# The second attention of a hybrid block: the last sums of squares of a group given later, the query tiles of a head from the longest down, and whole products in the last group

## The chip, the cores and the metric

The kernel runs on one core of a Trainium2 chip. The metric is the device time of one launch in microseconds, as the median of several runs. TensorE (PE in the profile) multiplies matrices into PSUM, VectorE (DVE), ScalarE (ACT) and GpSimd (POOL) work on vectors, SyncE (SP) starts the loads and stores. Each engine runs its own list of instructions in order and waits for others at semaphores.

## The reference

All is in fp32, with T = 1024 tokens of C = 512 channels. The block is four residual steps:

```
x = x + attention_a(layernorm(x))     # 32 heads of 16, rotary, causal
x = x + ffn(layernorm(x))             # base product, 2 of 8 low-rank experts
x = x + attention_b(layernorm(x))     # 32 query heads of 128, 8 key/value heads
x = x + ffn(layernorm(x))
```

Only attention B is changed. It computes

```
q = rmsnorm(x @ Wq.T) * qw            # 32 heads
k = rmsnorm(x @ Wk.T) * kw            # 8 heads, each for 4 query heads
v = x @ Wv.T
s = q k / sqrt(128) + slope * (key - query),  -1e30 where key > query
out = softmax(s) v;   result = out @ Wo.T
```

The mask is causal, so a query tile i (128 queries) sees the keys 0 to (i+1)*128: tile 7 is eight times as wide as tile 0.

## The kernel before

**Tiles and stages.** Attention B runs from about 500 to 1611 us of the profile. Its loop goes over 8 groups g (one key/value head each), 4 query heads hh of the group, and 8 query tiles i. For each tile:

- `softmax(g, hh, i)`: TensorE gives the scores s in one or two pieces of at most 512 keys (L791) into the pool `ps_s`, which has two PSUM buffers. VectorE multiplies each piece by the queries' norm factor rq and adds the distance (L793, "p"), takes the row maximum over the whole width (L797, "nm") and scales it (L798). ScalarE takes the exponent and its sum (L800), VectorE the reciprocal (L802), GpSimd scales p by it (L803).
- `columns(hh, p, i)`, two tiles later (`LAG = 2`): VectorE transposes p in 32x32 blocks, the first five key tiles into `PT` (L818, "pT") and the others into `TT` (L824, "tT"). `PT` is one buffer that all heads use; `TT` has a place for each of the four heads.
- `product(g, hh, i0, i1)`: TensorE multiplies the columns in PT of query tiles i0 to i1 by v, in matmuls that use 32 rows of the array each, four side by side (L835 through `by_groups`, "o"); ScalarE copies the result to oT (L860). It is called after the head's last tile.
- `product_rest(g, heads)`: the same for the key tiles 5 to 7 in TT, for several heads in one matmul ("or"), which VectorE adds to oT (L876). In groups 0 to 6 it is called once for all four heads, at the next group's start.

**What fills between.** While the softmax of group g goes on, TensorE is given the other work in small units. A generator `fill` yields after each: `project_kv(g+1)` makes keys and values of the next group in 8 units (four matmuls "kv" L700 each, then ScalarE's squares L708 and VectorE's copies k L709 and v L710), `project_o(g-1)` multiplies the previous group's oT by Wo and adds to x in 32 units (L642 "wo", addition L647), and `project_q(g+1)` makes the next group's queries in 32 units (L745 "pq"; ScalarE's squares L754, "qT" on VectorE L755), with one transposition of keys (L99 "tp_k", L728) between. All of these, and `sum_squares`, use the pool `ps_m` with two PSUM buffers.

`sum_squares(g, hh, sq)` sums the squares of a head's queries by four matmuls with ones (L771 "st"), transposes the sums on VectorE (L775 "by"), scales them (L779 "rq"), and takes the power on GpSimd. `project_q` calls it for head hh when it is two matmuls into head hh + 1, and for the last head at its own end, between two further yields.

**What sets the order.** After tile n of 32 the loop takes units of the fill until `done` reaches `due`, which is `units * n // 32`: an equal share for each tile, with `units` 74 (42 in group 0, which has no project_o). A scheduler then places the instructions of each engine, within what data and buffers allow, so that neighbours can change places. The last group has no next group: its fill is project_o(6) during heads 0 and 1, then project_o(7) for heads 0 and 1 together and for head 2; the last head's part of project_o runs inside the ffn that follows. In this group each head makes its product in two halves, tiles 0 to 3 when tile 3 is there and 4 to 7 when tile 7 is there, and its own product_rest.

Of the kernel before, what the change touches and what calls it, by code (L numbers as in the profile page):

```python
# [18 lines left out]
NT = T // P  # L19
# [16 lines left out]
HKV = 8  # L36
GRP = HB // HKV
# [27 lines left out]
class Block:  # L65
# [557 lines left out]
    def attention_b(self, ctx, wo_pool, WqT, WkT, WvT, WoT, qw, kw, xnT, missing, ffn_weights):  # L623
# [12 lines left out]
        oTs = {}  # L636
# [13 lines left out]
        with ExitStack() as ctx:  # L650
# [70 lines left out]
                        nc.gpsimd.tensor_scalar(k_sb[:, a, :], k_sb[:, a, :], rk[:, a : a + 1], 1.0, ALU.mult, ALU.mult)  # L721
                    later.append((g, half, k_sb, kT))

            later = []

            def k_columns(g, half, k_sb, kT):
                ps = self.transpose4(ps_m, [k_sb[:, a, :] for a in range(4)], f"k{g}{half}", tag="m")
                nc.scalar.activation(  # L728
                    kT[:, half * QC : (half + 1) * QC], ps.rearrange("p a b -> p (a b)"), AF.Copy, scale=kw_sb
                )  # L730

            def project_q(g, wq):

                qTs[g] = []
                rqs[g] = []
                sums = []
                for hh in range(GRP):
                    qT = qp.tile([P, T], F32, tag="qT", name=f"qT{g}_{hh}")
                    qTs[g].append(qT)
                    rqs[g].append(sm.tile([P, NT], F32, tag="rq", name=f"rq{g}_{hh}", bufs=6))  # L740
                    for qc in range(NQC):
                        cols = slice(qc * QC, (qc + 1) * QC)
                        ps = ps_m.tile([P, QC], F32, tag="m", name=f"pq{g}_{hh}_{qc}")
                        for kc in range(KC):
                            nc.tensor.matmul(  # L745
                                ps, lhsT=wq[:, kc, hh * DB : (hh + 1) * DB], rhs=xnT[:, kc, cols], start=(kc == 0), stop=(kc == KC - 1)
                            )
                            if kc < KC - 1:
                                yield
                            if kc == 1 and sums:  # L750
                                sum_squares(g, *sums.pop(0))
                        if qc == 0:
                            sq = work.tile([P, T], F32, tag="w", name=f"qsq{g}_{hh}", bufs=1)
                        nc.scalar.activation(sq[:, cols], ps, AF.Square)  # L754
                        nc.vector.tensor_scalar_mul(qT[:, cols], ps, qw_sb)  # L755
                        yield
                        while later:
                            k_columns(*later.pop(0))
                    sums.append((hh, sq))
                yield  # L760
                sum_squares(g, *sums.pop(0))
                yield

            def sum_squares(g, hh, squares):

                rq = rqs[g][hh]
                st = ps_m.tile([P, QC], F32, tag="m", name=f"st{g}_{hh}")[:, : NT * B]
                for a, sq in enumerate(squares.rearrange("p (i a c) -> a p i c", a=P // B, c=B)):  # L770
                    nc.tensor.matmul(  # L771
                        st[a * B : (a + 1) * B, :].rearrange("p (i c) -> p i c", c=B), lhsT=ones, rhs=sq, start=True, stop=True
                    )
                by_token = work.tile([P, NT, B], F32, tag="st", name=f"by{g}_{hh}", bufs=1)
                nc.vector.transpose(by_token.rearrange("p i c -> p (i c)"), st)  # L775


                s2 = slopes[g * GRP + hh] ** 2
                nc.vector.tensor_scalar(rq, by_token[:, :, 0], s2, DB * RMS_EPS * s2, ALU.mult, ALU.add)  # L779
                self.rsqrt(rq, rq, [NT])  # L780
# [62 lines left out]
            def queries(t, i0, i1):  # L843

                return t[:, i0 * P : i1 * P].rearrange("p (i a c) -> p a i c", a=NB, c=B)

            def product(g, hh, i0, i1):

                n = i1 - i0
                o = ps_o.tile([P, NB, QC], F32, tag="o", name=f"o{g}_{hh}_{i0}")  # L850
                by_groups(
                    g,
                    o,
                    lambda o, j: o[:, max(j - i0, 0) * B : n * B],
                    range(min(JS, i1)),
                    lambda j, rows, ks: PT[rows, (NT - 1) * j + max(j, i0) : (NT - 1) * j + i1, ks],
                )
                if i0 == 0:
                    oTs[g, hh] = otp.tile([P, T], F32, tag="oT", name=f"oT{g}_{hh}")
                nc.scalar.copy(queries(oTs[g, hh], i0, i1), o[:, :, : n * B].rearrange("p a (i c) -> p a i c", c=B))  # L860

            def product_rest(g, heads):

                n, h0 = len(heads), heads[0]
                o = ps_o.tile([P, NB, QC], F32, tag="o", name=f"or{g}_{h0}")
                by_groups(
                    g,
                    o,
                    lambda o, j: o[:, : n * JT * B].rearrange("p (h q) -> p h q", h=n)[:, :, (j - JS) * B :],
                    range(JS, NT),  # L870
                    lambda j, rows, ks: TT[rows, h0 : h0 + n, (JT - 1) * (j - JS) + j - JS : (JT - 1) * (j - JS) + JT, ks],
                )
                for h in heads:
                    to = queries(oTs[g, h], JS, NT)
                    more = o[:, :, (h - h0) * JT * B : (h - h0 + 1) * JT * B].rearrange("p a (i c) -> p a i c", c=B)
                    nc.vector.tensor_add(to, to, more)  # L876

            def in_turn(*gens):
                for g in gens:
                    yield from g  # L880
# [7 lines left out]
            heads = list(range(GRP))  # L888
            rest = []

            def finish(g, hh, i, p):
                while rest:
                    product_rest(*rest.pop(0))
                columns(hh, p, i)
                if g == HKV - 1:

                    if i == NT // 2 - 1:
                        product(g, hh, 0, NT // 2)
                    elif i == NT - 1:
                        product(g, hh, NT // 2, NT)  # L900
                        product_rest(g, [hh])
                elif i == NT - 1:
                    product(g, hh, 0, NT)
                    if hh == GRP - 1:
                        rest.append((g, heads))

            for g in range(HKV):


                last = g == HKV - 1  # L910
                parts = []
                if not last:
                    wq, wkv = load_qkv(g + 1)
                    parts.append(project_kv(g + 1, wkv))
                    parts.append(project_q(g + 1, wq))
                if g:
                    parts.insert(-1, project_o(g - 1, wo, heads, ps_m, "m"))
                fill = in_turn(*parts)
                units = 74 if g else 42
                done = 0  # L920
                for hh in range(GRP):
                    if g and hh == 2:
                        if last:
                            for _ in fill:
                                pass
                        wo = load_o(g)
                        if last:
                            fill = in_turn(project_o(g, wo, [0, 1], ps_m, "m"), project_o(g, wo, [2], ps_m, "m"))
                    for i in range(NT):
                        p = softmax(g, hh, i)  # L930
                        n = hh * NT + i + 1
                        if not last:
                            due = units * n // (GRP * NT)
                        elif hh < 2:
                            due = max(0, (n - 2) * 32 // 14)
                        else:
                            due = 32 + max(0, 2 * (n - 19)) if n < 27 else 48 + (n - 27)
                        while done < due:
                            next(fill, None)
                            done += 1  # L940
                        pending.append((g, hh, i, p))
                        if len(pending) > LAG:
                            finish(*pending.pop(0))
                    if last and hh == GRP - 1:
                        for item in pending:
                            next(fill, None)
                            finish(*item)
                for _ in fill:
                    pass
                if g == HKV - 2:  # L950

                    self.load_ffn(wp, nc.sync, ("wkv", "wq"), *ffn_weights)
# [156 lines left out]
```

## Time and profile before

| | |
|---|---|
| runs | 1683.14, 1683.34, 1686.43 us; median 1683.34 |
| profiled execution, its own time | 1683.11 us |
| its span in the trace | 1681.3 us |
| TensorE busy, share of the span | 1652.6 us, 98% |
| VectorE | 1103.0 us, 66% |
| ScalarE | 542.1 us, 32% |
| GpSimd | 347.8 us, 21% |
| L835 o and or, L745 pq, L791 s on the chain | 13% and 3%, 12%, 12% |
| product and rest records of L835 before the last group | 160 a head, 96 a group of four heads |

The span is what the trace covers, from the first instruction to the last; the launch's own time is a little longer. A busy TensorE is not TensorE at its peak: matmuls are pipelined, and the profile models their ends, so two rows of matmuls overlap a little. An fp32 matmul shows as two records. A timeline row gives start, length, engine and line, the operation with its output and inputs, how many records it holds, and in brackets the idle time before it with what ended that. A row of the waits gives the instruction that waited, the one that it waited for, total us, times, and the longest. A row of the groups by shape gives busy time, mean ns of one, and idle time before with what ended most of it.

### The profile page before, as it was taken

The page shows a single profiled execution, that of the slowest core. Times are in us where ns is not written, and L with a number is a line of the kernel's source. Part 1 is how long each engine was busy: PE and PEld are TensorE (multiplying, and loading weights), DVE is VectorE, ACT ScalarE, POOL GpSimd, SP SyncE. Part 2 cuts the span into 40 slices and gives each one's busy share as a digit, 9 for nine tenths or more (in the row PEclk, how much of TensorE's full clock was granted, in tenths as well). Part 3 has the DMA queues.
Part 4 walks back from the last instruction along what each step waited for, and adds up shares of the span by engine and source line. Part 5 has one row for each costly group of instructions (what it writes and reads, how often), then busy time and mean ns, then how long its engine had stood idle before and what let it go on. Part 6 is the DMA issues. An engine that isn't in the chain of part 4 may idle for free.

```text
span 1681.3 us, 32166 instructions
## 1 busy us (share of the span) xinstructions
PE 1652.6 (98%) x13016; PEld 940.7 (56%) x13016; DVE 1103.0 (66%) x2856; ACT 542.1 (32%) x1217; POOL 347.8 (21%) x508
## 2 busy tenths in 40 slices
PE   9999999999999999999999999999999999999988
PEld 5544444344555667556655665756655665566654
DVE  3556666662653886776677667676677766776773
ACT  2315555555111332233233223223223322322220
POOL 2000000000312332222123212222222321221140
PEclk9999999999999999999999999999999999999999
DMA  5000000001003201100200200110020020000001
GB/s 195 1 1 2 2 2 2 2 2 38 2 24 88 65 2 41 49 26 26 64 26 26 61 30 1 51 38 26 26 64 26 26 71 26 1 27 27 2 1 50
DMA packets 60868, 52.06 MB, mean 31 GB/s; under 512 B 5744, under 2 KB 47472, under 8 KB 60720
## 3 DMA queue, kind: packets, MB, share of 16 engines
q1 hardware_dynamic: 59408, 46.06, 9.2%
q0 software_dynamic: 784, 2.90, 0.4%
q8 instruction: 102, 1.67, 0.4%
q10 hardware_dynamic: 528, 1.05, 0.2%
q14 instruction: 46, 0.38, 0.1%
HBM read 30.98 MB, written 2.10 MB: 20 GB/s over the span
## 4 chain that ended last, share of the span: by engine, by line
PE 87%; DVE 10%; ACT 1%; POOL 1%; issue 1%; DVEq 0%; ACTq 0%; POOLq 0%
PE o L835 13%; PE pq L745 12%; PE s L791 12%; PE wo L642 9%; PE sT L354 7%; PE kv L700 7%; PE oT L389 5%; PE s L302 4%; PE pm_f L599 3%; PE or L835 3%; DVE p L793 3%; DVE nm L797 2%; DVE pT L818 2%; PE pj_v L179 2%; PE pm_ao L993 2%; PE pj_k L179 2%
## 5 line engine op out<-in xcount | busy, mean ns | idle before, releaser
L803 POOL TENSOR_SCALAR p<-p,rs 128x128 f32<-128x128 f32 (+7 forms) x256 | 190.8, 747 | 750.6 <-DVE rs L802 685.7
L800 ACT ACTIVATE p<-p,nm 128x128 f32<-128x128 f32 (+7 forms) x256 | 198.1, 774 | 453.4 <-DVE nm L798 443.0
L793 DVE SCALAR_TENSOR_TENSOR p<-s,rq,rel 128x512 f32<-128x512 f32 (+3 forms) x384 | 227.1, 605 | 119.4 <-PE s L791 118.8
L791 PE MATMUL s<-kT,qT 128*128 128x512 f32 (+3 forms) x768 | 294.8, 492 | 1.8 <-DVE p L793 1.5
L745 PE MATMUL pq<-xnTb,wq 128*128 128x512 f32 x512 | 246.2, 599 | 0.0
L642 PE MATMUL wo<-wo,oT 128*128 128x512 f32 x512 | 241.8, 594 | 3.4 <-DVE x L647 1.9
L791 PEld LDWEIGHTS s<-kT,qT 128*128 128x128 f32 x768 | 141.2, 190 | 165.8 <-issue 126.1
L835 PEld LDWEIGHTS o<-pT,va 32*128 32x128 f32 x5632 | 215.7, 185 | 28.5 <-DVE rs L802 11.8
L835 PE MATMUL o<-pT,va 32*128 32x128 f32 (+7 forms) x5632 | 224.6, 313 | 0.8
L818 DVE STREAM_TRANSPOSE pT<-p 128x640 f32<-128x640 f32 (+4 forms) x256 | 172.1, 673 | 73.1 <-PE o L835 54.7
L374 ACT ACTIVATE p<-sT 128x512 f32<-128x512 f32 (+1 forms) x320 | 157.5, 555 | 113.4 <-PE sT L372 70.9
L797 DVE TENSOR_REDUCE nm<-p 128x1 f32<-128x128 f32 (+7 forms) x256 | 188.2, 736 | 3.6
L302 PE MATMUL s<-kT,qT 32*128 32x512 f32 (+3 forms) x768 | 181.9, 522 | 0.0
L354 PE MATMUL sT<-qT,kT 32*128 32x512 f32 (+3 forms) x768 | 155.7, 521 | 0.0
L642 PEld LDWEIGHTS wo<-wo,oT 128*128 128x128 f32 x512 | 93.8, 190 | 87.5 <-issue 72.4
L745 PEld LDWEIGHTS pq<-xnTb,wq 128*128 128x128 f32 x512 | 92.3, 190 | 87.9 <-issue 80.2
L700 PE MATMUL kv<-wkv,xnTb 128*128 128x256 f32 x512 | 116.7, 382 | 4.4 <-DVE nm L798 4.0
L700 PEld LDWEIGHTS kv<-wkv,xnTb 128*128 128x128 f32 x512 | 95.8, 190 | 26.2 <-DVE nm L798 6.9
L319 DVE TENSOR_REDUCE part<-s 128x1 f32<-128x512 f32 x128 | 80.8, 684 | 40.6 <-PE s L302 36.0
L354 PEld LDWEIGHTS sT<-qT,kT 32*128 32x128 f32 x768 | 60.5, 183 | 62.2 <-issue 24.0
L860 ACT COPY oT<-o 128x1024 f32<-128x1024 f32 (+1 forms) x36 | 33.0, 916 | 181.8 <-PE o L835 176.6
L302 PEld LDWEIGHTS s<-kT,qT 32*128 32x128 f32 x768 | 76.4, 183 | 25.7 <-ACT p L374 10.3
(153 smaller groups left out, 1610.4 us busy)
## 6 DMA issues: line engine op xcount, KB each, us to landing
va<-v SPq DMA_DIRECT2D x256, 64.0 KB
wq<-in_b_WqT_dram SPq DMA_DIRECT2D x8, 1024.0 KB
wo<-in_b_WoT_dram SPq DMA_DIRECT2D x8, 1024.0 KB
x<-in_x_dram SPq DMA_DIRECT2D x8, 256.0 KB
wkv<-in_b_WkT_dram SPq DMA_DIRECT2D x8, 256.0 KB
wkv<-in_b_WvT_dram SPq DMA_DIRECT2D x8, 256.0 KB
out_dram<-x SPq DMA_DIRECT2D x8, 256.0 KB
wq<-in_a_wqT_dram ACTq DMA_DIRECT2D x1, 1024.0 KB
```

Of the source, the lines that this page charges most:

```text
L302: nc.tensor.matmul(made[j][:, at:end], lhsT=qT[rows_of(j), c, i * P : (i + 1) * P], rhs=kT[rows_of(j), c, kc * QC : kc * QC + end - at], s ...
L354: nc.tensor.matmul(made[j][:, at:end], lhsT=kT[rows_of(j), c, b * P : (b + 1) * P], rhs=qT[rows_of(j), c, (qc + 1) * QC - (end - at) : (qc ...
L642: nc.tensor.matmul(ps, lhsT=oTs[g, h][:, t * P : (t + 1) * P], rhs=wo[:, h, :], start=(h == heads[0]), stop=(h == heads[-1]))
L700: nc.tensor.matmul(ps.rearrange("p a b -> p (a b)"), lhsT=xnT[:, kc, i * P : (i + 1) * P], rhs=wkv[:, kc].rearrange("p a b -> p (a b)"), s ...
L745: nc.tensor.matmul(ps, lhsT=wq[:, kc, hh * DB : (hh + 1) * DB], rhs=xnT[:, kc, cols], start=(kc == 0), stop=(kc == KC - 1))
L791: nc.tensor.matmul(s, lhsT=qT[:, i * P : (i + 1) * P], rhs=kT[:, lo:hi], start=True, stop=True)
L793: nc.vector.scalar_tensor_tensor(p[:, lo:hi], s, rq[:, i : i + 1], rel[:, at + lo : at + hi], ALU.mult, ALU.add)
L797: nc.vector.tensor_reduce(nm, p[:, :w], AX.X, ALU.max, negate=True)
L800: nc.scalar.activation(p[:, :w], p[:, :w], AF.Exp, bias=nm, scale=slope, accum_out=ss)
L803: nc.gpsimd.tensor_scalar(p[:, :w], p[:, :w], rs, 1.0, ALU.mult, ALU.mult)
L818: nc.vector.transpose(PT[:, i : i + (NT - 1) * (m - 1) + 1 : NT - 1, :], p[:, : m * P].rearrange("p (j k) -> p j k", k=P))
L835: nc.tensor.matmul(cols(o[:, a], j), lhsT=vs[g][rows, j * NB + b, :], rhs=moving(j, rows, slice(b * B, (b + 1) * B)), start=(j == js[0] an ...
```

## The change

It has three parts.

1. `project_q` no longer gives the last head's sum_squares at its end with two yields. It puts the call on a list `owed`, and the next group's loop makes it when two units of its own fill are done (`done == 2`).
2. A head's tiles run from 7 down to 0 (`down`), except in the last head of the last group. The product follows tile 0. The fill is shared out not equally but by `SHARE`, a weight for each tile index (24 for tile 0, 70 for tile 5, 42 for tiles 6 and 7; sum 368). `units` are 72 and 40, as two yields are gone.
3. In the last group, heads 0 to 2 make one whole product each; heads 0 and 1 have one product_rest together, after head 1, and head 2 one of its own. The last head keeps its halves and its order.

```diff
@@ project_q
                     sums.append((hh, sq))
-                yield
-                sum_squares(g, *sums.pop(0))
-                yield
+                owed.append(lambda: sum_squares(g, *sums.pop(0)))
@@ product
-                if i0 == 0:
+                if (g, hh) not in oTs:
                     oTs[g, hh] = otp.tile([P, T], F32, tag="oT", name=f"oT{g}_{hh}")
@@ finish
+            down = list(reversed(range(NT)))
+            SHARE = [24, 34, 42, 54, 62, 70, 42, 42]
             def finish(g, hh, i, p):
                 while rest:
                     product_rest(*rest.pop(0))
                 columns(hh, p, i)
-                if g == HKV - 1:
+                last = g == HKV - 1
+                if last and hh == GRP - 1:
                     if i == NT // 2 - 1:
                         product(g, hh, 0, NT // 2)
                     elif i == NT - 1:
                         product(g, hh, NT // 2, NT)
                         product_rest(g, [hh])
-                elif i == NT - 1:
+                elif i == 0:
                     product(g, hh, 0, NT)
-                    if hh == GRP - 1:
+                    if last and hh:
+                        product_rest(g, heads[:2] if hh == 1 else [hh])
+                    elif not last and hh == GRP - 1:
                         rest.append((g, heads))
@@ the loop over groups
-                units = 74 if g else 42
-                done = 0
+                units = 72 if g else 40
+                done = share = 0
-                    for i in range(NT):
+                    for at, i in enumerate(range(NT) if last and hh == GRP - 1 else down):
                         p = softmax(g, hh, i)
-                        n = hh * NT + i + 1
+                        n = hh * NT + at + 1
                         if not last:
-                            due = units * n // (GRP * NT)
+                            share += SHARE[i]
+                            due = units * share // (GRP * sum(SHARE))
@@
                         while done < due:
                             next(fill, None)
                             done += 1
+                            if done == 2:
+                                while owed:
+                                    owed.pop(0)()
```

More of the change, by code (lines that the diff above doesn't have):

```diff
@@ L722, in project_kv @@
                     later.append((g, half, k_sb, kT))
-            later = []
+            later, owed = [], []
             def k_columns(g, half, k_sb, kT):
```

## The prediction

> **What bounds the kernel now.** I read the page's busy times and chain first, then the waits of TensorE, then the timeline at the places that those waits name, then the groups by shape.
>
> ```profile
> PE 1652.6 (98%) x13016; PEld 940.7 (56%) x13016; DVE 1103.0 (66%) x2856; ACT 542.1 (32%) x1217; POOL 347.8 (21%) x508
> ...
> PE 87%; DVE 10%; ACT 1%; POOL 1%; issue 1%; DVEq 0%; ACTq 0%; POOLq 0%
> ```
>
> TensorE carries the chain; its clock row is all nines. [...] Inside attention B one group follows another every 138.77 us (kv starts 918.27 and 1057.04 below). By spacing of starts, a group's matmuls cost: s 31.8, pq 27.5, wo 27.5, kv 13.8, four products 27.0, one joint rest 5.4, and st, tp_k and switches of form the remaining 5.8 less one stall of 0.88. That fills the period: in groups 1 to 6 TensorE is full, and each matmul's start spacing removed is time removed. [...]
>
> ```profile
> PE kv L700 <- DVE nm L798: 4.0, 5, 0.8
> PE wo L642 <- DVE x L647: 1.9, 2, 1.3
> ...
> PE s L791 <- DVE p L793: 1.5, 3, 0.7
> PE wo L642 <- DVE nm L798: 1.4, 2, 0.8
> ```
>
> Columns: total, times, longest. The first row is the end of a group:
>
> ```profile
> 914.92 1.02 PE L745 MATMUL pq<-xnTb,wq 128*128 128x512 f32 x2
> 915.78 1.12 PE L791 MATMUL s<-kT,qT 128*128 128x128 f32 x4
> 916.82 0.64 PE L771 MATMUL st<-qsq,ones 128*32 128x256 f32 x8
> 918.27 1.56 PE L700 MATMUL kv<-wkv,xnTb 128*128 128x256 f32 x6 [0.81 <-DVE nm L798]
> ...
> 1057.04 0.48 PE L700 MATMUL kv<-wkv,xnTb 128*128 128x256 f32 x1 [0.81 <-DVE nm L798]
> ```
>
> ```profile
> 916.38 1.18 DVE L797 TENSOR_REDUCE nm<-p 128x1 f32<-128x1024 f32 x1
> 917.48 0.73 DVE L755 TENSOR_SCALAR qT<-pq,qw_sb 128x512 f32<-128x512 f32 x1
> 918.13 0.14 DVE L798 TENSOR_SCALAR nm<-nm 128x1 f32<-128x1 f32 x1
> ```
>
> kv0 needs one of two PSUM buffers; st has one, the last pq the other, and (VectorE's timeline) its reader qT stands behind the 1.18 us reduction of tile 7, the longest tile, which ends the head. st to kv0 is 918.27 - 916.82 = 1.45 us; unstalled, after group 0, it is 640.00 - 639.43 = 0.57. Stall: 0.88 us, at five boundaries into kv and once (1472) into wo.
>
> **Part 1 and the boundary.** sum_squares of head 3 (8 st records, by, rq, a POOL power) is only moved behind two fill units of the next group; no DMA is issued by it, and no queue of SP is passed. Now the head ends on tiles 2, 1, 0. The order becomes s7 (two), kv0, kv1, st, s6. Counted from the end of the last pq: VectorE is through qT after about 1.7, so kv0 and kv1 (wanted at 1.7 and 3.45) are free. st reuses kv0's buffer: wanted at 2 x 0.86 + 2 x 1.73 = 5.2, while VectorE has to give two 741 ns p, a pT, the 1.12 us reduction, k0, nm and v0 first, about 4.95. No stall, with only 0.25 us to spare; kv2 and kv6 have 0.65 and 0.7. rq of head 3 is due three heads later. Five boundaries: **-4.4** (the sixth is counted below). If the cover fails it is st that stalls, by tenths.
>
> **Part 2, longest first.** It adds no instruction. What it brings: the first two tiles of a head, 7 and 6, have their pT written while the product of the previous head still reads the one PT, so VectorE waits for the product's end and is then behind. Today the short tiles do that wait (groups by shape in attention B: busy, mean ns, idle before and its releaser; rows in no order of time):
>
> ```profile
> L818 DVE STREAM_TRANSPOSE pT<-p 128x640 f32<-128x640 f32 x128 | 107.0, 836 | 6.8 <-POOL p L803 5.7
> ...
> L818 DVE STREAM_TRANSPOSE pT<-p 128x128 f32<-128x128 f32 x32 | 9.9, 311 | 19.2 <-PE o L835 19.2
> ...
> L793 DVE SCALAR_TENSOR_TENSOR p<-s,rq,rel 128x512 f32<-128x512 f32 x192 | 140.5, 741 | 50.2 <-PE s L791 49.7
> ```
>
> After the product come two pT (about 0.77 each), then tile 5's p (0.74): tile 4's s has its bank 2.3 us after the product, and TensorE wants it after two fill units and s5, at 3.2 to 4.0. Margin 0.9 to 1.8: I take **0** for groups 1 to 6, with 0 to +1 us a head as bounds. The work that hides it is the fill; without fill it costs the whole 2.3. Group 0 is that case in part: it has 40 units and not 72, a head lasts some 25 us against about 19 of softmax alone on VectorE plus 3 to 7 of fill. There I walk out 0.15 a head, and at 0->1 about 2.0 (s7 waits for p of tile 1, kv2 for qT, st for v0 behind the reduction), in all **+2.3** (0.5 to 4).
>
> **Part 3, the last group.** Three of four heads get one product each and heads 0 and 1 a joint rest. First TensorE's timeline (start, length), then its groups by shape:
>
> ```profile
> 786.75 6.80 PE L835 MATMUL o<-pT,va 32*128 32x256 f32 x160
> ...
> 1513.33 4.86 PE L835 MATMUL o<-pT,va 32*128 32x128 f32 x160
> ...
> 1554.32 2.88 PE L835 MATMUL or<-tT,va 32*128 32x96 f32 x96
> ...
> 1563.13 3.77 PE L835 MATMUL o<-pT,va 32*128 32x128 f32 x128
> ```
>
> ```profile
> L835 PE MATMUL o<-pT,va 32*128 32x128 f32 x1504 | 49.0, 272 | 0.1
> ...
> L835 PE MATMUL o<-pT,va 32*128 32x96 f32 x128 | 4.2, 267 | 0.0
> ...
> L835 PE MATMUL o<-pT,va 32*128 32x32 f32 x128 | 4.2, 268 | 0.0
> ```
>
> A timeline row counts to the end of the last record, so I cost by the spacing of starts: a quartet of records, one for each 32 rows, of 256, 224, 192, 160 and 128 columns takes 0.216, 0.189, 0.162, 0.136 and 0.109 us, and 8 quartets go to each key tile. Whole product 8 x 0.812 = 6.50 (row: 6.73 to the next start, 0.20 of it the change of form). Second half 8 x 5 x 0.109 = 4.36. [...] Rests: 2 x 2.62 (3 x 8 x 0.109 each) against a joint one of 8 x (0.162 + 0.109 + 0.109) = 3.04: 2.2. Four fewer changes of form, 0.09 into, 0.20 out and 0.105 on the next record by the spacings: 1.6. Together **-7.85** of TensorE time. Old stalls gone: 0.88 (1472), 0.72 + 0.31 (1545), 0.44 (1591): **-2.35**. New ones: project_o(6) of tile 0 waits for the four rest additions of group 6 behind tile transposes, 0.85; the first wo of heads 0 and 1 waits for the joint rest's additions, 1.4: **+2.25** (1 to 5). The last head keeps its order and its four stalls of 1600 to 1611. Sum: -7.95.
>
> ACT copies fall from 36 to 33 (1.0 us each, hidden); loads on SP keep their places. x additions are the same in number.
>
> **Sum.** -4.4 + 0 + 2.3 - 7.95 = **-10.1 us**. The profiled execution has span 1681.3 and 1683.11 in all (1.8 around it); 1671.2 + 1.8 = 1673.0. The median shown is 0.2 above it: **1673.2**.
>
> **Rivals.** (A) The boundary's stall moves and does not go: st waits for v0 behind tile 7's reduction, now in each group, and group 0 costs its 4. For it: 0.25 us of margin. Against: VectorE is at 66%. Then 1683.3 - 8 + 4 = 1679.3. (B) In the last group VectorE's softmax sets the end: the stalls from 1600 on are already its own, and less matmul work only widens them. Against: before 1600 the last group shows only 2.35 us of stalls in 125. Then the 8 shrink to about 3, half of what is left after 2 us of the new waits: 1683.3 - 4.4 + 2.3 - 3 = 1678.2; with A as well 1683.3 + 4 - 3 = 1684, no change. (C) Slower: the wait for PT. VectorE waits out the 6.8 us product at the head of its queue, behind it stand qT or x additions that free the fill's two buffers, and tiles 5 and 4. If that starves TensorE after each of some 28 products, the price is 28 times the loss: from 0.36 us a head (10.1 / 28) it eats all gain, at 0.7 it is 1673.2 + 19.6 = 1692.8. For it: VectorE's row of 50 us idle on s shows that it is fed, not that it has reserve within a head. Against: the margins above. (D) The change doing nothing is excluded in the last group, where 480 matmul records fewer are issued.
>
> **How the numbers follow.** The likeliest case 0.62 (own range 1667 to 1678: group 0 from 0.5 to 4, new stalls 1 to 5, less a gain of up to 2 where fewer waits come than walked); A or B alone 0.15 (1677 to 1681); both together 0.06 (around 1684); C 0.17 (1681 to 1695). This kernel can tell 0.2%, 3.4 us, from no change: faster is below 1680.0. Faster 0.62 + 0.13 = 0.75, same 0.08, slower 0.17. The range leaves out a little of C's end: 1665 to 1688.
>
> **What would show it.** Right: no stall of kv behind st at the five boundaries; kv starts some 137.9 us apart; product records of 128 columns fewer by 480 or so and no idle TensorE over 1 us in groups 1 to 6; the last group some 8 us shorter. Wrong: a row of s waiting for p of 10 us or more, idle TensorE after each product (C); st waiting for v (A); the stalls near the end grown from 3.9 to 8 (B); group 0 longer by over 4.

## The result, and the profile after

The changed kernel takes 1674.64 us (median; 1673.22 to 1674.99) against 1684.05 for the kernel before in the same runs: a ratio of 0.9941, with a 95% interval of 0.9928 to 0.9955. That is 9.4 us faster; forecast were 1673.2 us and 10.1 us. The profiled execution has a span of 1672.5 us against 1681.3.

The sum was right within 0.7 us of the gain, but not each of its terms. First the busy times and the chain of the page of after:

```profile
PE 1647.0 (98%) x12536; PEld 935.6 (56%) x12536; DVE 1114.0 (67%) x2856; ACT 543.0 (32%) x1214; POOL 347.3 (21%) x508
...
PE 95%; DVE 3%; ACT 1%; POOL 1%; issue 0%; DVEq 0%; ACTq 0%; POOLq 0%
```

TensorE issues 480 records fewer. VectorE's part of the chain has gone from 10% to 3%, with the same 2856 instructions. That is not 7% of the time: TensorE's idle time in the span fell only from 28.7 us (1681.3 - 1652.6) to 25.5 us (1672.5 - 1647.0). TensorE's waits after (total us, times, longest):

```profile
PE wo L642 <- DVE nm L798: 3.1, 1, 3.1
PE tp_g_f L99 <- DVE g_f L584: 2.6, 1, 2.6
...
PE s L791 <- DVE p L793: 1.8, 3, 1.1
...
PE wo L642 <- DVE rs L802: 0.9, 1, 0.9
...
PE kv L700 <- DVE qT L755: 0.5, 1, 0.5
```

The row of kv waiting for nm (4.0 us, five times) is gone. New is one wait of 3.1 us, in the last head of the last group. A boundary between groups after, on TensorE's timeline and then on VectorE's:

```profile
915.30 1.88 PE L745 MATMUL pq<-xnTb,wq 128*128 128x512 f32 x4
917.02 1.88 PE L791 MATMUL s<-kT,qT 128*128 128x512 f32 x4
918.73 3.62 PE L700 MATMUL kv<-wkv,xnTb 128*128 128x256 f32 x16
922.32 0.64 PE L771 MATMUL st<-qsq,ones 128*32 128x256 f32 x8
```

```profile
918.09 0.75 DVE L755 TENSOR_SCALAR qT<-pq,qw_sb 128x512 f32<-128x512 f32 x1
918.76 1.40 DVE L793 SCALAR_TENSOR_TENSOR p<-s,rq,rel 128x512 f32<-128x512 f32 x2
920.08 0.30 DVE L818 STREAM_TRANSPOSE pT<-p 128x128 f32<-128x128 f32 x1
920.30 1.18 DVE L797 TENSOR_REDUCE nm<-p 128x1 f32<-128x1024 f32 x1
...
921.88 0.29 DVE L710 COPY v<-kv 128x128 f32<-128x128 f32 x1
```

qT now stands ahead of the 1.18 us reduction. v0 ends at 922.17 and st starts at 922.32: its spacing from kv is 0.04 us more than in a place where nothing waits. The forecast saw 0.25 us to spare; there is none, but also no stall worth the name.

I compare the kernels at four marks of TensorE, in the profiled executions (us from the span's start; the start of the last record of pq for group 2, then for group 7, of the last rest, and of all matmuls). The queries of a group are made during the group before, so the five boundaries from group 1 to group 6 lie between the first two marks:

| | pq for group 2 | pq for group 7 | last rest | last matmul |
|---|---|---|---|---|
| before | 776.58 | 1470.42 | 1620.09 | 1676.61 |
| after | 779.28 | 1465.80 | 1609.97 | 1667.83 |
| stretch before | | 693.84 | 149.67 | 56.52 |
| stretch after | | 686.52 | 144.17 | 57.86 |
| change | +2.70 | -7.32 | -5.50 | +1.34 |

The steady groups follow one another every 137.30 us, not 138.77. The end of the last head of the last group, first TensorE's timeline, then the stretches with the clock in the column after POOL:

```profile
1587.49 1.98 PE L791 MATMUL s<-kT,qT 128*128 128x512 f32 x4
1589.31 1.88 PE L642 MATMUL wo<-wo,oT 128*128 128x512 f32 x4
1594.29 2.08 PE L642 MATMUL wo<-wo,oT 128*128 128x512 f32 x2 [3.10 <-DVE nm L798]
1597.24 4.46 PE L642 MATMUL wo<-wo,oT 128*128 128x512 f32 x6 [0.87 <-DVE rs L802]
```

```profile
1590.00:1595.00 5.00, 1.90 (x4) 0.69 (x3) 4.86 (x8) 0.60 (x1) 0.00 (x0) 0.87 0.00 0
1595.00:1600.00 5.00, 4.13 (x6) 1.25 (x5) 1.44 (x4) 0.64 (x2) 1.12 (x1) 0.50 0.00 0
...
1630.00:1635.00 5.00, 4.16 (x10) 2.01 (x11) 1.93 (x7) 0.00 (x0) 0.00 (x0) 0.66 0.00 0
```

While TensorE sat idle, its clock fell to half; the records after 1597.24 are some 0.85 us apart until it comes back, where 0.43 is usual. The same happens once more in the ffn, at 1631. In the profile before, the clock is 1.00 up to the last matmul.

What TensorE waited for at 1594.29 stands on VectorE's timeline: wo takes one of the two buffers of `ps_m`, and the additions to x that free them (L647) come behind p and the reduction of tile 7:

```profile
1591.02 1.37 DVE L793 SCALAR_TENSOR_TENSOR p<-s,rq,rel 128x512 f32<-128x512 f32 x2
1592.42 1.22 DVE L797 TENSOR_REDUCE nm<-p 128x1 f32<-128x1024 f32 x1
1593.56 0.68 DVE L647 TENSOR_TENSOR x<-x,wo 128x512 f32<-128x512 f32 x1
```

### The profile page after: what moved, and what is told of

Same layout as the page of the kernel before. It is cut to its first block, busy times and chain, and to the rows that moved or that the text cites. A ratio compares the mean times of both kernels' runs of the same rounds, so it can differ in the third digit from the quotient of the medians.

```text
span 1672.5 us, 31107 instructions
## 1 busy us (share of the span) xinstructions
PE 1647.0 (98%) x12536; PEld 935.6 (56%) x12536; DVE 1114.0 (67%) x2856; ACT 543.0 (32%) x1214; POOL 347.3 (21%) x508
## 4 chain that ended last, share of the span: by engine, by line
PE 95%; DVE 3%; ACT 1%; POOL 1%; issue 0%; DVEq 0%; ACTq 0%; POOLq 0%
PE s L791 15%; PE pq L745 13%; PE o L835 13%; PE wo L642 13%; PE sT L354 7%; PE kv L700 7%; PE oT L389 5%; PE s L302 4%; PE pm_f L599 3%; PE or L835 3%; PE pj_v L179 2%; PE pm_ao L1007 2%; PE pj_k L179 2%; PE sT L372 1%; PE pj_q L179 1%; PE st L771 1%
## 5 line engine op out<-in xcount | busy, mean ns | idle before, releaser
L800 ACT ACTIVATE p<-p,nm 128x1024 f32<-128x1024 f32 (+7 forms) x256 | 198.2, 774 | 410.2 <-DVE nm L798 367.8
L803 POOL TENSOR_SCALAR p<-p,rs 128x1024 f32<-128x1024 f32 (+7 forms) x256 | 190.4, 745 | 653.9 <-DVE rs L802 629.8
L835 PEld LDWEIGHTS o<-pT,va 32*128 32x128 f32 x5248 | 210.8, 185 | 25.5 <-issue 17.9
L835 PE MATMUL o<-pT,va 32*128 32x256 f32 (+5 forms) x5248 | 220.0, 321 | 0.0
L797 DVE TENSOR_REDUCE nm<-p 128x1 f32<-128x1024 f32 (+7 forms) x256 | 189.0, 738 | 3.0
L389 PE MATMUL oT<-p,v_p 128*32 128x256 f32 (+3 forms) x1024 | 87.4, 417 | 0.0
```

Of the source, the lines that this page charges most:

```text
L389: nc.tensor.matmul(o[rows_of(j), QC - w + x0 : QC - w + x1], lhsT=v_cols(b, c * HC + j), rhs=p[:, j, at + x0 : at + x1], start=first, stop ...
L797: nc.vector.tensor_reduce(nm, p[:, :w], AX.X, ALU.max, negate=True)
L800: nc.scalar.activation(p[:, :w], p[:, :w], AF.Exp, bias=nm, scale=slope, accum_out=ss)
L803: nc.gpsimd.tensor_scalar(p[:, :w], p[:, :w], rs, 1.0, ALU.mult, ALU.mult)
L835: nc.tensor.matmul(cols(o[:, a], j), lhsT=vs[g][rows, j * NB + b, :], rhs=moving(j, rows, slice(b * B, (b + 1) * B)), start=(j == js[0] an ...
```

## The experiments

My theory at the start: a boundary's stall goes through both the order of tiles and the moved sums; group 0 loses because it has too little fill; the wait for PT is hidden; the last group gains its products and gives part back through VectorE and the clock. Times are medians, beside those of the kernel before on the same chip.

### Part 1 alone

```diff
 # the kernel before
-                yield
-                sum_squares(g, *sums.pop(0))
-                yield
+                owed.append(lambda: sum_squares(g, *sums.pop(0)))
```

(with the pop at `done == 2`, and 72 and 40 units.)

> Part 1 alone: the last head's sums of squares of a group are given after two fill units of the next group; tiles still run 0 to 7 with equal shares, the last group keeps its halves. Theory (buffer queue): kv0 finds a free buffer and kv1 is wanted about when qT behind the 1.18 us reduction is through, so 0.6 to 1.5 us go at each of six boundaries: 1683.9 - 4 to 9, some 1675 to 1680. Rival (the descending order is what removes the stall, since the reduction of tile 7 stays ahead of qT): the stall only moves to kv1 or st, 1682 to 1684.

Measured: 1685.81 against 1684.65, ratio 1.0012 (1.0005 to 1.0019). It makes the kernel a little slower. The rival was right that the stall only moves, but not to kv1 or st, and the time lies above its range too. The waits of TensorE show the new place:

```profile
PE tp_k L99 <- ACT kT L728: 4.4, 7, 0.9
```

The stall of kv behind st is gone (kv follows at once), but by spacing of starts the key transposition now waits 0.74 us a group instead of 0.22, and the records of the four products take 27.5 us of a group's spacing instead of 26.9, because the scheduler starts a product and interleaves kv with it. The period is 138.93 us. Taking a stall out at one place is worth nothing while VectorE's order stays what it was.

### Without part 1

```diff
 # the changed kernel
-                owed.append(lambda: sum_squares(g, *sums.pop(0)))
+                yield
+                sum_squares(g, *sums.pop(0))
+                yield
```

(74 and 42 units.)

> The changed kernel without part 1: sums of squares again at the end of project_q, descending tiles, shares and whole products kept. Theory: the short tiles at the head's end let qT through about 1.7 us after the last pq, kv0 is wanted at about 1.4, so 0.3 us a boundary come back: 1674.6 + 2, about 1676.5. Rival (part 1 carries the gain of the boundary): the full 1.47 us of a group's period comes back six times, 1683.

Measured: 1680.43 against 1684.65, ratio 0.9979 (0.9971 to 0.9987), between the two numbers, and neither held. The period is 138.37 us, so 1.07 of the 1.47 us come back:

```profile
PE kv L700 <- DVE qT L755: 3.0, 6, 0.6
```

kv now waits for qT itself, 0.57 us at each of the five boundaries (the row's sixth, 0.17, is behind group 0): kv0 is wanted right behind st, and that is too early even with short tiles at the head's end. Descending tiles need the moved sums as much as the sums need them.

### Equal shares

```diff
 # the changed kernel
-            SHARE = [24, 34, 42, 54, 62, 70, 42, 42]
+            SHARE = [1] * NT
```

> The changed kernel with an equal share of the fill for each tile, descending. Theory (TensorE is full while the fill covers the long tiles): the long tiles 5 to 3 get 2.25 units for 3.4 to 2.6, VectorE needs about 3.2 us a tile against some 3.6 of TensorE, so little is lost: 0 to 0.4 us a head over 28 heads, 1675 to 1686. Rival C (no reserve within a head): 0.7 us or more a head, above 1692.

Measured: 1683.66 against 1684.65, ratio 0.9997 (0.9989 to 1.0005): without the weights nearly all the gain is gone. It lies in the theory's range, but not by its mechanism, a loss spread over the heads. The period is 138.73, and 1.03 of the 1.43 us lost in it by spacing of starts have one place, here on the timeline (idle time in brackets):

```profile
921.18 3.62 PE L700 MATMUL kv<-wkv,xnTb 128*128 128x256 f32 x16
925.75 0.64 PE L771 MATMUL st<-qsq,ones 128*32 128x256 f32 x8 [0.96 <-DVE v L710]
```

With equal shares the short tiles carry more fill, VectorE comes to the first tile of the next head later, and v0 is given behind its reduction: st waits for it. This is rival A of the prediction, in the kernel without SHARE. What SHARE buys there is that VectorE is ahead at the boundary. Some 2.2 us more go from the last pq to the last rest (146.36 us against 144.17). SHARE with ascending tiles was not run.

### The last group as before

```diff
 # the changed kernel
-                if last and hh == GRP - 1:
+                if last:
...
-                    for at, i in enumerate(range(NT) if last and hh == GRP - 1 else down):
+                    for at, i in enumerate(range(NT) if last else down):
```

(halves, and a rest for each head, in the whole last group.)

> The changed kernel with its last group as before: tiles 0 to 7, two half products and a rest for each head. Theory: the last group's 5.5 us come back, and the 1.3 us that the changed kernel loses behind it (clock at half after a TensorE idle time of 3.1 us) go: 1674.6 + 5.5 - 1.3, about 1679; clock 1.00 throughout. Rival (the last group gained nothing by its products, VectorE sets its end): 1674 to 1676.

Measured: 1678.43 against 1684.65, ratio 0.9967 (0.9954 to 0.9979): parts 1 and 2 alone are worth 6.2 us, and about 3.2 us less is gained than by the full change. The theory's 1679 holds, but not its two terms. From the last pq to the last rest it takes 148.08 us, 3.9 more than in the changed kernel and not 5.5: the other 1.6 (149.67 - 148.08) are parts 1 and 2 at the boundary into the last group. And the 1.3 us behind do not go: from the last rest to the last matmul it takes 58.21 us, where after had 57.86 and before 56.52. The ffn has a spell at half clock here as well, though no idle time of 3.1 us comes ahead of it:

```profile
1633.92:1637.33 3.41, 1.61 (x8) 0.78 (x7) 2.72 (x16) 0.00 (x0) 0.00 (x0) 1.00 0.00 0
1637.33:1640.74 3.41, 3.41 (x8) 1.80 (x7) 0.69 (x1) 0.59 (x1) 0.00 (x0) 0.50 0.03 5
```

### Part 3 alone

```diff
 # the kernel before, in finish
-                if g == HKV - 1:
+                last = g == HKV - 1
+                if last and hh == GRP - 1:
...
                 elif i == NT - 1:
                     product(g, hh, 0, NT)
-                    if hh == GRP - 1:
+                    if last and hh:
+                        product_rest(g, heads[:2] if hh == 1 else [hh])
+                    elif not last and hh == GRP - 1:
```

> The kernel before with part 3 alone: heads 0 to 2 of the last group make whole products, heads 0 and 1 one rest; tiles run 0 to 7 throughout and the sums of squares stay. Theory (the 7.85 us of TensorE time are taken from the path whatever the order of tiles): 1683.8 less 4 to 7, 1677 to 1680. Rival (ascending, the whole product has to wait for the widest tile, and project_o of heads 0 and 1 for it): 1682 to 1687.

Measured: 1675.79 against 1683.49, ratio 0.9947 (0.9930 to 0.9963), better than the theory. The stretch from the last pq to the last rest is 141.41 us (before 149.67, after 144.17), and that with the boundary's stall still in it. So 7.7 us for part 3 alone and 6.2 for parts 1 and 2 alone, but 9.4 for all: 4.5 us are lost between them. (In the profiles, from the last pq to the last rest: 8.26 and 1.59 alone, 5.50 together, so 4.35.) The stalls ahead of the last half product are 2.9 us of it: by spacing of starts, records at half clock among them, they sum to 4.2 us here, 3.9 before and 7.1 after. Where the rest goes was not traced. After, the heads 0 to 2 descend and the last head ascends, so that two runs of short tiles meet and then the widest tiles come last; that this order is the reason is argued, not shown. VectorE is busy only 11.37 of the 20 us from 1560 to 1580, and sets the pace right behind it.

### Group 0 ascending

```diff
 # the changed kernel
-                elif i == 0:
+                elif i == (0 if g else NT - 1):
...
-                            share += SHARE[i]
+                            share += SHARE[i] if g else sum(SHARE) // NT
```

(and its tiles run 0 to 7.)

> The changed kernel with group 0 alone in the order of before: tiles 0 to 7, equal shares, 40 units. Theory (group 0 has too little fill for longest first): the 2.8 us that the trace shows as lost up to the second group come back in part, the boundary 0 to 1 then ends on tile 7 as in the run of part 1 alone: 1674.6 - 1.5 to 2.8, about 1672.5. Rival (the loss has another cause, such as the boundary): 1674 to 1676.

Measured: 1671.46 against 1683.63, ratio 0.9927 (0.9912 to 0.9942), 12.2 us below the kernel before instead of 9.4. The first mark is at 776.71, where before had 776.58 and after 779.28. So longest first, with its shares, costs 2.6 us in group 0 and behind it, and the boundary 0 to 1 costs nothing against before even when tile 7 ends the head there.

### The wait for PT taken away

```diff
 # the changed kernel
+            scr = ptp.tile([P, JS, P], F32, tag="scr", name="scr")
+            nc.gpsimd.memset(PT, 0.0)
                 nc.vector.transpose(
-                    PT[:, i : i + (NT - 1) * (m - 1) + 1 : NT - 1, :], p[...]
+                    scr if i >= 6 else PT[:, i : i + (NT - 1) * (m - 1) + 1 : NT - 1, :], p[...]
```

> The changed kernel with the transposes of tiles 7 and 6 (first five key tiles) going to a scratch tile and not to PT, so that they no longer wait for the product of the head before; the columns of these tiles in PT stay zero, so their outputs leave these keys out. Theory (the wait of VectorE for PT is covered by the fill): TensorE's period of 137.30 us in groups 1 to 6 stays within 0.1, time within 2 us of the changed kernel. Rival C (the wait costs time in each head): 0.2 us or more a head, 5 us or more faster, below 1669.

Measured: 1666.70 against 1683.63, ratio 0.9903 (0.9889 to 0.9918). By its time alone this would be rival C's. The period says otherwise: it is 137.30 us, the same as after to a hundredth. VectorE's groups by shape in attention B, after and then here:

```profile
L793 DVE SCALAR_TENSOR_TENSOR p<-s,rq,rel 128x512 f32<-128x512 f32 x192 | 139.4, 732 | 16.6 <-PE s L791 15.4
L818 DVE STREAM_TRANSPOSE pT<-p 128x640 f32<-128x640 f32 x128 | 104.6, 834 | 97.9 <-PE o L835 83.2 <-POOL p L803 12.5
```

```profile
L793 DVE SCALAR_TENSOR_TENSOR p<-s,rq,rel 128x512 f32<-128x512 f32 x192 | 140.3, 740 | 92.8 <-PE s L791 91.5
L821 DVE STREAM_TRANSPOSE scr<-p 128x640 f32<-128x640 f32 x64 | 53.8, 841 | 31.5 <-POOL p L803 31.3
```

VectorE's 83 us of waiting for the product turn into 76 us more of waiting for the next scores: TensorE is the one that is waited for either way. The gain lies elsewhere, and the edit made it by accident: the second half product of the last head no longer depends on tiles 6 and 7, so it starts ahead of them. The last record of head 2's product starts at 1568.90 after and at 1567.66 here; the last record of the last head's second half goes from 1606.11 to 1594.36, and in this profile the clock stays at 1.00 up to the last matmul. So the run settles the steady groups; its total says nothing of them.

### Work in the idle place

```diff
 # the changed kernel, after tile 7 of the last head
+                            busy = ps_o.tile([P, NB, QC], F32, tag="o", name="busy")
+                            for _ in range(4):
+                                nc.tensor.matmul(busy[:, 0, :], lhsT=kTs[g][:, :P], rhs=kTs[g][:, :QC], start=True, stop=True)
```

> The changed kernel with four 128x512 matmuls added (3.4 us, their result is not read) where TensorE is idle for 3.1 us in the last head. Theory (that idle time drops TensorE's clock to half for the next 5 us): the clock stays at 1.00 around 1595, the wo after it last 0.43 us a record again, and the kernel is 1 to 3 us faster in spite of more matmuls, 1672 to 1673.5. Rival (the row of the clock has no weight, VectorE sets the pace there): same or 0.5 us slower.

Measured: 1673.77 against 1683.63, ratio 0.9941 (0.9926 to 0.9956), about 0.5 us better than after: less than the theory asked, and too near the rival for the time to decide. The stretches decide on the clock:

```profile
1590.00:1595.00 5.00, 4.50 (x11) 1.71 (x9) 3.64 (x6) 1.20 (x2) 0.00 (x0) 1.00 0.00 0
1595.00:1600.00 5.00, 3.65 (x90) 2.85 (x94) 3.22 (x6) 0.04 (x1) 1.12 (x1) 1.00 0.01 3
```

It stays at 1.00, and the last record of the last half product starts 4.2 us earlier (1601.95 against 1606.11). But the last matmul is only 0.6 us earlier: in the ffn behind it the clock falls at 1618 and again at 1631 (after: once), and the wait for g_f grows to 3.37 us of spacing from 2.80. What the end of attention B gains, the start of the ffn gives back.

### The last head descending too

```diff
 # the changed kernel
-                if last and hh == GRP - 1:
-                    ... halves at tiles 3 and 7, then the rest
-                elif i == 0:
+                if i == 0:
                     product(g, hh, 0, NT)
...
-                    for at, i in enumerate(range(NT) if last and hh == GRP - 1 else down):
+                    for at, i in enumerate(down):
```

> The changed kernel with the last head of the last group also from tile 7 down, one whole product and one rest. Theory (VectorE is behind at the end because the long tiles come last): the 7 us of stalls between 1587 and 1601 go, the last product is 2 us longer after its last tile: 1674.6 - 2 to 5, about 1671. Rival (the order of the last head is right: the whole product has to wait for the last tile, and nothing is left to fill the wait): 1675 to 1681.

Measured: 1672.50 against 1683.63, ratio 0.9932 (0.9916 to 0.9949), some 1.7 us better than after, just short of the theory's 2. The stalls become smaller ones for x (0.9, 1.3, 0.9, 0.4), but the rest waits 1.39 us for ScalarE's copy of the whole product, and the clock is at half from 1602 to 1609.

### Both, and then Wo's parts joined

```diff
 # group 0 ascending and the last head descending
 # then, in both of the joined kernels:
-                            fill = in_turn(project_o(g, wo, [0, 1], ps_m, "m"), project_o(g, wo, [2], ps_m, "m"))
+                            fill = project_o(g, wo, [0, 1], ps_m, "m")
-                            due = 32 + max(0, 2 * (n - 19)) if n < 27 else 48 + (n - 27)
+                            due = 32 + max(0, (n - 18) * 16 // 13)
-        return lambda ps_m: project_o(HKV - 1, wo, [GRP - 1], ps_m, "pm")
+        def last_heads(ps_m):
+            for n, _ in enumerate(project_o(HKV - 1, wo, [GRP - 2, GRP - 1], ps_m, "pm")):
+                if n % 2:
+                    yield
+        return last_heads
```

> The changed kernel with group 0 ascending at equal shares and the last head of the last group descending with one product, the two edits that gained each by itself. Theory (they lie 900 us apart and add): 1674.3 - 2.6 - 2, about 1669.5 to 1670. Rival (the last head's gain depends on the state in which it is reached): 1671.5 to 1673.

Measured: 1667.51 against 1683.49, ratio 0.9901 (0.9886 to 0.9916). It is 2 us better than the sum of the two, so theory and rival both missed. The same 1.39 us wait ahead of the rest is there, but this time the clock does not fall behind it (1.00 from 1600 to 1610): from the last rest to the last matmul it takes 60.11 us, where the run with only the last head descending took 62.59.

> As the run with group 0 up and the last head down, and Wo's part of head 2 of the last group is taken together with head 3's in the ffn that follows, so that x gets 8 additions of 0.68 us fewer; the fill of heads 0 and 1 is spread over heads 2 and 3. Theory (VectorE sets the end of the last group): up to 5.4 us go in head 3, and TensorE's 6.9 us of moved work fill part of the ffn's 8 us of stalls: 1666 to 1669. Rival (the moved matmuls lengthen the ffn): 1670 to 1674.

Measured: 1669.66 against 1683.49, ratio 0.9916 (0.9901 to 0.9931), between the two expectations. The last rest comes 4.1 us earlier than in the run before it (1596.56 against 1600.64), but the ffn waits 5.6 us for g_f, and the last matmul is 1.6 us later.

> Group 0 up and Wo's part of head 2 joined with head 3's, but the last head ascending in two half products as in the changed kernel. Theory: the third wo of head 2 no longer stalls 3.1 us behind the reduction of tile 7 and the clock stays at 1.00 up to 1610; VectorE still has the widest tiles last: 1667 to 1670. Rival: as before it, 1671 to 1673.

Measured: 1665.15 against 1683.49, ratio 0.9885 (0.9870 to 0.9900): 18.3 us faster than the kernel before, better than the changed kernel by about 9, and below both expectations. The end of its last group:

```profile
1581.06 1.88 PE L791 MATMUL s<-kT,qT 128*128 128x512 f32 x4
1584.40 6.28 PE L642 MATMUL wo<-wo,oT 128*128 128x512 f32 x14 [1.46 <-DVE p L793]
```

One idle place of 1.46 us is left where after had 3.1 and 0.87, and the clock stays at 1.00 until 1620. Then the ffn waits for g_f again (4.1 us of spacing) and runs four records at half clock. With one whole product (the run before) TensorE is idle for 2.9 us at the same place.

## Why the prediction was right

**The bound.** That TensorE is full in groups 1 to 6 holds: less TensorE work and fewer stalls came out as time, and the run without the wait for PT left the period as it was, 137.30 us.

**The boundary.** Forecast -4.4 for five of them; measured -7.32 for the five periods. The mechanism was right, but the term was mis-sized: I counted only the spacing from st to kv. By spacing of starts, around it lay more of the same: the scores just ahead of st came 0.19 us late, the records behind these two stalls lost 0.10 each, a kv pair 0.14, and one change from wo to a product cost 0.29 where 0.09 is usual. With the 0.88 that is 1.6 us; a tenth is spent elsewhere after the change, 0.04 of it at st, and 1.47 is the period's gain. The runs add what the text did not say, read from the period of 138.77 before: the moved sums alone give 138.93, the order with its shares but without the moved sums 138.37, order and sums with equal shares 138.73, all three 137.30. Rival A was not far: the margin at st was nothing rather than 0.25, and equal shares are enough to bring it about, with 1.03 us and not "tenths".

**Longest first.** 0 for groups 1 to 6: shown by the run that takes the wait away. Rival C's place was real, 83 us of VectorE's idle time, and its price zero. Group 0: +2.3 forecast, +2.7 by the marks, 2.6 back in the run that undoes it. Its split was less good. Against that run, 1.0 us goes up to the last pq in group 0 and 1.3 behind it, where the text had 0.15 a head (0.45 to 0.6 in all) and about 2.0; these terms add to some 2.5, not 2.3.

**The last group.** Forecast -7.95, measured -5.50. The matmul work was costed well: the joint rest runs from 1541.64 to the next start at 1544.88, 3.24 us, that is 3.04 and the change of form of 0.20, and the product records of 128 columns fall from 1504 to 1024. Of the 7.85 us, 4.05 (7.85 - 2.2 - 1.6) stand for three whole products in place of halves, 1.35 each. The rows show the term: before, a first half takes 3.70 us to the next start (1563.13 to 1566.83) and a second 4.68 (1580.13 to 1584.81); after, a whole product takes 6.72 (1533.43 to 1540.15). That is 1.66 a head, with the cost of one change of form in it. The step that failed is "The last head keeps its order and its four stalls of 1600 to 1611": they are 7.1 us instead of 3.9. Of the new stalls only one came, 1.28 us instead of 2.25. So -7.85 - 2.35 + 1.3 + 3.2 = -5.7, against -5.5 measured. This is rival B, in part: VectorE sets the end there. TensorE gives the scores of tile 7 13.9 us earlier than before (1587.49 against 1601.36), VectorE reduces them 13.1 us earlier (1592.42 against 1605.54), and the additions that free wo's buffers stand behind that. Part 3 alone, with tiles ascending, keeps the stalls at 4.2, and the run in which head 2's wo is given later (halves kept) has one idle place of 1.46 us.

**Behind it.** Forecast 0, measured +1.34 up to the last matmul: 0.5 us more idle time of the ffn's three waits (6.2 against 5.7), and some 1.5 us of three to four records at half clock; the rest of that sum was made up elsewhere in the ffn. But the half clock in the ffn is not the change's alone. The two kernels that keep their ffn's waits as before, the last group as before and part 3 alone, have it in their profiles too (58.21 and 58.22 us, where before and part 1 alone, without it, have 56.52 and 56.55), and most executions of the kernel before have a mean clock below 1.000, though a timing does not show where: of its 41 beside the first four experiments, 10 have a mean granted clock of 1.000 and take 1683.15 us on average, 27 have 0.999 and take 1684.58, and 4 have 0.998 and take 1685.33. The profile of before, on which the sum was built, has 1.000.

So the sum of -10.1 came out by luck in its size: a boundary gain too small by 2.9 met a last group too large by 2.5 and a loss of 1.3 that was not seen. Where the gain would come from was right; what each place gives was not.

## What to carry to other kernels

A stall at a full engine can be more than its row in the waits (here 0.81 us in the row, 1.47 in the period): compare the whole period of a loop. One edit can move the stall: here only the order of tiles, the place of the sums and the shares of the fill together took it away (137.30 us, against 138.37 to 138.93 with one or two of them). When an engine gets less work near the end, ask who arrives late there: here 5.50 of the 7.95 us forecast came out, with VectorE's widest tiles last. The 83 us that VectorE waited for TensorE's products cost nothing, as TensorE was the full one; take such a wait away in a steady loop and read the period, not the total. And a profile is one execution: before 1 or 2 us at the end are put down to a change, compare its clock with that of the other timings.

## What the hardware showed that was not expected

TensorE's clock fell to half within attention B and the ffn after waits, and their length alone does not decide. After, an idle time of 3.1 us brings 0.50 in the next 5 us, and with work put into that place it stays at 1.00. In the kernel before, three idle times of 1.67 to 1.82 us in the ffn leave the clock at 1.00; in the run with only the last head descending, an idle time of 1.12 us between two products is followed by half clock for 6.8 us, and in the run that adds the edit of group 0, 900 us earlier, the same one is not.

In the trace of after, TensorE's clock is at half twice ahead of the last matmul, from 1593.74 to 1600.56 us and from 1631.28 to 1634.69: for 6.83 and 3.41 us, and the 30.72 us between them are nine times 3.41. With stretches of 3.41 us cut at these edges, the one ahead of each fall shows what TensorE did (its busy time comes first behind the length):

```profile
1590.33:1593.74 3.41, 0.86 (x3) 0.03 (x1) 3.38 (x6) 0.00 (x0) 0.00 (x0) 1.00 0.00 0
1593.74:1597.15 3.41, 2.08 (x2) 0.50 (x2) 1.90 (x5) 1.24 (x2) 0.00 (x0) 0.50 0.00 0
...
1627.87:1631.28 3.41, 0.77 (x4) 0.40 (x3) 3.07 (x18) 0.00 (x0) 0.00 (x0) 1.00 0.00 0
1631.28:1634.69 3.41, 3.41 (x7) 1.49 (x7) 0.72 (x2) 0.00 (x0) 0.00 (x0) 0.50 0.00 0
```

TensorE was busy for 0.25 of the stretch ahead of the first fall and for 0.23 of that ahead of the second. Cut in the same way, no other stretch of this trace from 20 us to the last matmul was busy for less than 0.60. In the kernel before (cut at the one fall, 5.9 us behind the start of its last matmul), the emptiest are those from 1627.89 and 1634.72 us, busy for 0.51 and 0.50, and the clock behind them stays at 1.00. Why half clock follows the idle time of 1.12 us in one run and not in the other stays open. No run moved a wait on purpose; only that filling the wait of 3.1 us keeps the clock was tested.
